# An accumulation of exponentials put behind the background piece of its step

## The chip, the cores and the metric

The kernel runs on one core of one Trainium2 chip. The metric is the device time of one execution in microseconds; less is better. The kernel before took 2945.7 us (median of three runs, 2944.8 to 2946.02).

## The reference, cut to what matters

Four layers of attention over images of 64 x 64 positions with 64 channels, four images, all in fp32. Layer 0 normalises over the keys and sums over the queries, layer 1 has 8 channels for keys and queries and pools its keys, and layers 2 and 3 are the ones that the change touches. Both begin with a group norm, have 4096 queries and 4096 keys per image, and end with a projection and a residual:

```python
# layer 2
q = linear_last(xn, Wq, bq); k = linear_last(xn, Wk, bk); v = linear_last(xn, Wv, bv)
w = jnp.einsum('bchw,bcHW->bhwHW', q, k) * scale
w = jax.nn.softmax(w.reshape(B, H, W, H * W), axis=-1).reshape(B, H, W, H, W)
out = linear_last(jnp.einsum('bhwHW,bcHW->bchw', w, v), Wp, bp) + residual
# layer 3
attn = jnp.einsum('bhwc,bHWc->bhwHW', q, k) * scale
attn = jax.nn.softmax(attn.reshape(B, H, W, H * W), axis=-1).reshape(B, H, W, H, W)
out = h + (jnp.einsum('bhwHW,bHWc->bhwc', attn, v) @ wp + bp)
```

The softmax needs the sum of the exponentials over the keys for each query. That sum, before it is folded over partitions, is what the line of the change computes.

## The kernel before, in words

**Units and steps.** `attention` (L1271) does layers 2 and 3 of one image. It has NC = 4 chunks c of queries times NB = 32 blocks j of keys, 128 units u. `first(u)` (L1282) lets TensorE compute the scores of a unit into an `s` buffer of 128 x 1024 in PSUM (L1287), ScalarE take the exponential into a buffer `p` in SBUF (L1292), and VectorE add `p` to the running sum `zacc` of the chunk (L1298); for j = 0 there is nothing to add. `then(u)` (L1314), two steps later or more, multiplies `p` with the values into two accumulators in PSUM (L1322). At the end of a chunk ScalarE copies one accumulator (L1331) and VectorE adds the other (L1332). There are two `s` buffers, four accumulators, and 14 `p` buffers, used in rotation.

**Order by hand.** The schedule is manual: each engine's instructions stand in the order in which Python issues them. A step (L810) does two units: it calls `first(2t)` and `first(2t+1)`, then the first `then` that is due, then `advance(MID)` (L819), then the second `then`, in the midst of which it may call `advance(LATE)`; then it issues what was put into the list `later`, and last `advance(END)`. `first` issues the add of the odd unit into `later`, and that of the even unit at once. So the order on VectorE within a step is: the even unit's add, the MID piece, the sum of accumulators if there is one, and out of `later` the odd unit's add and, at the end of a chunk, the transpose of `zacc` (L1306) and its reduction (L1310).

**Background pieces.** While the attention of one image runs, the preparation of another runs behind it, cut into pieces by generators that yield the place at which the next piece may go: MID, ALONE, LATE or END. `background` (L779) starts such a generator with a tempo, which is added to a credit in each step; a piece costs one credit (`ready`, L794, and `advance`, L800). The preparation of layer 0 is `before0`, of layer 2 `before2` (its normalising pieces and L1418, L1438 with their evacuations L1423 and L1443), of layer 3 `before3` (means and variances by `summed`, L1353 and L1354, the square L1498 that ScalarE takes of what VectorE wrote in L1496, the projection and the values L906 and L910). Layer 1 as a whole (`layer1`, L1060) is such a background: its score units go to LATE (L1118, L1124) with their own accumulation on VectorE (L1133), its beginning and end to MID and ALONE. A piece that uses TensorE takes one of the two `s` buffers, so that the scores of a later unit wait until the piece's result has been read out of it.

**Urgent pieces.** The end of each chunk puts two entries into `urgent`: `turn` (sums over partitions by L1241, L1246 and L1249, transpose and division L1261 with L1254 or L1268), two steps later, and `last` (layer 2: projection L1466 and residual L1472; layer 3: L1531, L1542 and the stores), two or four steps after it. `advance(MID)` takes an urgent entry that is due ahead of any other piece, and then no LATE piece goes into that step.

**Stages.** After a first stage the order is: layer 0 of image 1 with layers 1 and 2's preparation of image 0; layer 2 of image 0 with layer 1 of image 1; and so on. In the profile the eight stages of layers 2 and 3 begin at 531.7, 1030.9 and 1530.4 us (layer 2, with layer 1 of the next image behind them), 1803.8 and 2028.6 (layer 3), 2255.9 (layer 2), 2481.6 and 2708.4 (layer 3, the last without background).

Of the kernel before, what the change touches and what calls it, by code (L numbers as in the profile page):

```python
# [597 lines left out]
def fast_path(tc: tile.TileContext, a: dict, out: bass.AP, bad, read_flag):  # L598
# [21 lines left out]
    MID, ALONE, LATE, END = range(4)  # L620
# [152 lines left out]
    now = [0]  # L773
    due, before, urgent = {}, {}, []
    later = []
# [18 lines left out]
    def ready(place):  # L794
        at = back["at"]
        if place == LATE and back["alone"] == now[0]:
            return False
        return back["credit"] >= 1.0 and (at == place or place == MID and at == ALONE)

    def advance(place):  # L800
        if place == MID and urgent and urgent[0][0] <= now[0]:
            back["alone"] = now[0]
            urgent.pop(0)[1]()
        elif ready(place):
            if back["at"] == ALONE:
                back["alone"] = now[0]
            back["credit"] -= 1.0
            back["at"] = next(back["gen"], None)

    def step(first=None):  # L810
        back["credit"] = min(back["credit"] + back["tempo"], 3.0)
        for f in before.pop(now[0], ()):
            f()
        if first is not None:
            first()
        work = due.pop(now[0], [])
        for n, f in enumerate(work[:2]):
            if n == 1:
                advance(MID)  # L819
            split = n == 1 and ready(LATE)  # L820
            f(lambda: advance(LATE)) if split else f()
        for f in work[2:]:
            f()
        if len(work) < 2:
            advance(MID)
            advance(LATE)
        passes = list(later)
        later.clear()
        for f in passes:
            f()  # L830
        advance(END)
        now[0] += 1
# [7 lines left out]
    def parts(within, whole):  # L840

        if within is None or whole:
            yield slice(0, 512)
            if within is not None:
                within()
        else:
            yield slice(0, 256)
            within()
            yield slice(256, 512)
# [406 lines left out]
    def turn(o, zsums, spread):  # L1256


        t = o_tile("turned") if spread is None else p_tile()[:, 0:512]
        r = sums(zsums)[1]  # L1260
        nc.vector.transpose(t, o)  # L1261
        if spread is None:
            divide(blocked(t), t, r)
            return t
        u = o_tile("turned")
        split = lambda t: t.rearrange("p (j n f) -> p j n f", n=2, f=32)
        r = r.rearrange("p (j n) -> p j n", n=2).unsqueeze(3).to_broadcast([P, 8, 2, 32])
        nc.vector.tensor_tensor(u.rearrange("p (n j f) -> p j n f", n=2, f=32), split(t), r, ALU.mult)  # L1268
        return spread(u)

    def attention(st, last, not_before, name, final=None, spread=None):  # L1271

        q, k, v = st.pop("q"), st.pop("k"), st.pop("v")
        ps, accs, zaccs, zsums, os = {}, {}, {}, {}, {}
        pairs = NC * NB // 2  # L1280

        def first(u):  # L1282
            c, j = divmod(u, NB)
            s = s_tile()
            for i in range(2):
                for e in range(2):
                    nc.tensor.matmul(  # L1287
                        s[half(e), chunk(i)], k[(j + i) % 2][half(i), ds(j // 2 * P + e * C, C)], q[half(i), chunk(c)],
                        start=True, stop=True,
                    )  # L1290
            p = ps[u] = p_tile()
            nc.scalar.activation(p, s, AF.Exp)  # L1292
            if j == 1:
                zaccs[c] = z_p.tile([P, 1024], FP, tag="zacc", name="zacc")
            if j >= 1:

                p0 = ps[u - 1] if j == 1 else zaccs[c]
                add = lambda: nc.vector.tensor_tensor(zaccs[c], p0, p, ALU.add)  # L1298
                later.append(add) if j % 2 else add()
            if j == NB - 1:  # L1300
                later.append(lambda: turn_blocks(c))

        def turn_blocks(c):

            t = p_tile()
            nc.vector.transpose(t, zaccs.pop(c))  # L1306

            def sum_blocks():
                zsums[c] = small.tile([P, 32], FP, tag="zsums", name="zsums")
                nc.vector.tensor_reduce(zsums[c], t.rearrange("p (n k) -> p n k", k=32), AX.X, ALU.add)  # L1310

            later.append(sum_blocks)

        def then(u, within=None):  # L1314
            c, j = divmod(u, NB)
            if j == 0:
                accs[c] = [acc_tile() for _ in range(2)]
            p = ps.pop(u)
            for cols in parts(within, j in (0, NB - 1)):
                for e in range(2):  # L1320
                    for i in range(2):
                        nc.tensor.matmul(  # L1322
                            accs[c][e][half(i), cols], v[half(e), j, :], p[half(e), chunk(i)][:, cols],
                            start=(j == 0), stop=(j == NB - 1),
                        )
            if c == NC - 1 and j == NB - 1 and final is not None:
                final(accs.pop(c), zsums.pop(c))
            elif j == NB - 1:
                o = os[c] = o_tile("o")
                acc = accs.pop(c)  # L1330
                nc.scalar.copy(o, acc[0])  # L1331
                nc.vector.tensor_tensor(o, o, acc[1], ALU.add)  # L1332
                urgent.append((now[0] + 2, lambda: os.update({c: turn(os[c], zsums.pop(c), spread)})))
                end = now[0] + (4 if spread is None else 6)
                urgent.append((end, lambda: last(c, os.pop(c))))
                if c == NC - 1:
                    urgent.append((end, lambda: st.update({name: True})))

        start = now[0]
        for t in range(pairs):  # L1340
            g = max(start + t + 2, not_before + t // 2)
            due.setdefault(g, []).extend([lambda *within, u=u: then(u, *within) for u in (2 * t, 2 * t + 1)])
        for t in range(pairs):
            step(lambda: (first(2 * t), first(2 * t + 1)))
        return 0
# [493 lines left out]
def conv_seq_kernel(tc: tile.TileContext, a: dict, out: bass.AP):  # L1839

    nc = tc.nc
    with tc.tile_pool(name="flag", bufs=1) as flag:
        bad = flag.tile([1, 1], I32, name="bad")
        n_bad = fast_path(tc, a, out, bad, lambda: nc.values_load(
            bad[0:1, 0:1], min_val=0, max_val=128, skip_runtime_bounds_check_because="it is a count of 128 partitions"
        ))
        with tc.If(n_bad > 0):
            general_path(tc, a, out)
# [37 lines left out]
```

## Time and profile before

| | |
|---|---|
| median of three runs | 2945.7 us |
| the profiled execution | 2945.29 us |
| its span, first to last instruction | 2943.1 us |
| mean granted clock of TensorE | 0.999 |
| TensorE busy | 2910.0 us, 99% |
| VectorE busy | 1843.0 us, 63% |
| ScalarE busy | 1925.2 us, 65% |
| GpSimd busy | 33.6 us, 1% |
| DMA | 30.12 MB, mean 10 GB/s |
| stages of layer 2 with layer 1 behind | 273.4 to 273.8 us each |
| other stages of layers 2 and 3 | 224.8 to 227.3 us, the last 234.6 with the end |

PE stands for TensorE's matmuls, PEld for its weight loads, DVE for VectorE, ACT for ScalarE, SP for SyncE. L1298 is line 1298 of the kernel. A group is given as line, engine, operation, result and inputs; its columns are busy time, mean duration in ns, and the idle time of the engine before it with what ended most of that. The table of waits gives, for an engine and line, what it waited for, and then microseconds in total, times, and the longest. A timeline line is start, duration, engine, line, operation; a bracket at its end is the idle time before it. The ends of matmuls are modelled[...], so that short gaps of TensorE are better seen from the starts.

### The profile page before, as it was taken

To read this page: it belongs to the slowest core of one execution; us is meant where nothing else is said; L and a number is where in the kernel's file an instruction comes from. 1 tells how busy PE (TensorE), PEld (TensorE's weight loads), DVE (VectorE), ACT (ScalarE), POOL (GpSimd) and SP (SyncE) were. 2 spreads that over 40 slices of the span, in tenths; PEclk is the share of its full clock that TensorE was granted. 3 is DMA by queue.
4 is the path that set the end of the run, shared out by engine and by line. 5 is a ranking of instruction groups with operands and counts; after the bars stand their busy time and mean duration, and the time that the engine had idled before them with its cause. 6 is when DMAs were issued, how large, how long until landed. Compare 5 with 4: busy or idle time off the path is not lost.

```text
span 2943.1 us, 66611 instructions
## 1 busy us (share of the span) xinstructions
PE 2910.0 (99%) x29349; PEld 1147.8 (39%) x29349; DVE 1843.0 (63%) x2112; ACT 1925.2 (65%) x2769; POOL 33.6 (1%) x32
## 2 busy tenths in 40 slices
PE   9999999999999999999999999999999999999998
PEld 3333235333544433444443334333344344333333
DVE  1211742588731078872017888888988878878877
ACT  6877777665588866567886665555555555555554
POOL 0000000000000000000000000000000000000000
PEclk9999999999999999999999999999999999999999
DMA  2010000000001000000000000000000100000000
GB/s 38 1 30 5 1 2 13 8 5 17 8 5 30 1 5 5 20 7 17 1 1 5 5 22 6 19 5 9 5 19 6 22 5 8 6 19 5 9 5 10
DMA packets 76779, 30.12 MB, mean 10 GB/s; under 512 B 70465, under 2 KB 74561, under 8 KB 75073
## 3 DMA queue, kind: packets, MB, share of 16 engines
q1 hardware_dynamic: 74224, 25.37, 4.6%
q8 instruction: 232, 3.80, 0.5%
q10 hardware_dynamic: 2256, 0.41, 0.1%
q14 instruction: 67, 0.54, 0.1%
HBM read 4.79 MB, written 4.19 MB: 3 GB/s over the span
## 4 chain that ended last, share of the span: by engine, by line
PE 96%; DVE 2%; ACT 1%; issue 0%; DMA 0%; ACTq 0%; DVEq 0%
PE acc L1322 29%; PE s L1287 29%; PE s L994 15%; PE acc L1025 15%; PE s L1118 2%; PE acc L1144 2%; DVE zacc L1298 1%; ACT p L1124 1%; PE s L1144 1%; PE s L906 1%; PE s L1418 0%; PE s L885 0%; PE s L1179 0%; PE s L1090 0%; PE s L1438 0%
## 5 line engine op out<-in xcount | busy, mean ns | idle before, releaser
L1292 ACT ACTIVATE p<-s 128x1024 f32<-128x1024 f32 x1024 | 994.9, 1022 | 684.3 <-PE s L1287 655.6
L1298 DVE TENSOR_TENSOR zacc<-zacc,p 128x1024 f32<-128x1024 f32 x960 | 1173.6, 1222 | 288.1 <-ACT p L1292 240.5
L1322 PE MATMUL acc<-p,v 64*64 64x512 f32 (+1 forms) x8576 | 1017.8, 572 | 0.0
L1322 PEld LDWEIGHTS acc<-p,v 64*64 64x64 f32 x8576 | 347.7, 133 | 541.7 <-issue 541.7
L1025 PE MATMUL acc<-p,vs 64*64 64x512 f32 (+1 forms) x4224 | 513.3, 578 | 0.5 <-ACT vs L1014 0.5
L1004 ACT ACTIVATE p<-s 128x1024 f32<-128x1024 f32 x480 | 487.3, 1016 | 35.0 <-PE s L994 16.2
L1287 PE MATMUL s<-q,k 64*64 64x512 f32 x2048 | 499.4, 590 | 1.7 <-ACT p L1124 1.7
L994 PE MATMUL s<-xT,q 64*64 64x512 f32 x2048 | 488.5, 591 | 3.0 <-DVE v L910 0.9
L994 PE MATMUL s<-xT,q_swapped 64*64 64x512 f32 x2048 | 489.1, 591 | 0.7 <-DVE o L1153 0.7
L1287 PE MATMUL s<-q,xT 64*64 64x512 f32 x2048 | 488.8, 590 | 0.0
L1287 PE MATMUL s<-q,h_swapped 64*64 64x512 f32 x2048 | 480.2, 589 | 1.8 <-DVE mean L1354 0.5
L1287 PE MATMUL s<-q,k_swapped 64*64 64x512 f32 x2048 | 477.7, 590 | 0.1
L1006 DVE TENSOR_REDUCE all_z<-z 128x1 f32<-128x4 f32 x128 | 20.1, 157 | 624.3 <-ACT p L1004 624.0
L1025 PEld LDWEIGHTS acc<-p,vs 64*64 64x64 f32 x4224 | 186.6, 133 | 262.0 <-issue 198.6
L1014 ACT ACTIVATE vs<-v,all_r 64x64 f32<-64x64 f32 x512 | 176.8, 345 | 138.8 <-PE acc L1025 70.4
L994 PEld LDWEIGHTS s<-xT,q_swapped 64*64 64x64 f32 x2048 | 149.8, 133 | 143.7 <-issue 109.5
L1287 PEld LDWEIGHTS s<-q,k_swapped 64*64 64x64 f32 x2048 | 149.1, 133 | 135.1 <-issue 89.0
L1287 PEld LDWEIGHTS s<-q,h_swapped 64*64 64x64 f32 x2048 | 145.2, 133 | 142.4 <-issue 128.5
L1287 PEld LDWEIGHTS s<-q,xT 64*64 64x64 f32 x2048 | 145.3, 133 | 138.0 <-issue 130.2
L994 PEld LDWEIGHTS s<-xT,q 64*64 64x64 f32 x2048 | 149.1, 133 | 126.9 <-issue 95.6
L1287 PEld LDWEIGHTS s<-q,k 64*64 64x64 f32 x2048 | 150.0, 133 | 113.3 <-issue 92.0
L1124 ACT ACTIVATE p<-s 128x1024 f32<-128x1024 f32 x128 | 124.2, 1022 | 80.8 <-PE s L1118 80.8
(218 smaller groups left out, 1315.1 us busy)
## 6 DMA issues: line engine op xcount, KB each, us to landing
k_swapped<-k SPq DMA_DIRECT2D x8, 512.0 KB, 5.4
residual<-turned SPq DMA_DIRECT2D x128, 32.0 KB, 1.8
h_swapped<-xT SPq DMA_DIRECT2D x8, 512.0 KB, 5.8
out_dram<-turned SPq DMA_DIRECT2D x60, 64.0 KB, 2.0
xin<-in_x_dram SPq DMA_DIRECT2D x12, 256.0 KB, 6.6
q_swapped<-q SPq DMA_DIRECT2D x6, 512.0 KB, 5.9
pg<-pg SPq DMA_DIRECT2D x8, 128.0 KB, 2.3
xin<-in_x_dram SPq DMA_DIRECT2D x12, 64.0 KB, 2.3
```

The source lines that it names most:

```text
L906: nc.tensor.matmul(s[half(e), ds(i * 512 + k * C, C)], rhs[half(i), ds((g * 8 + k) * P + e * C, C)], w[half(i), half(i)], start=True, stop ...
L994: nc.tensor.matmul(s[half(e), chunk(i)], queries(m, i, e), k[half(i), chunk(c)], start=True, stop=True)
L1004: nc.scalar.activation(p, s, AF.Exp, accum_out=z)
L1014: nc.scalar.activation(vs[half(e), :], v[half(e), m, :], AF.Copy, scale=rz[half(e), m : m + 1])
L1025: nc.tensor.matmul(acc[c][half(i), cols], vs[half(e), :], ps[2 * t + n][half(e), chunk(i)][:, cols], start=(m == 0 and e == 0), stop=(m == ...
L1118: nc.tensor.matmul(ss[e][half(m), chunk(i)], pgs[0 if e == d else 1][r, ds(n * P + m * C, C)], th[r, chunk(i ^ j)], start=True, stop=True,)
L1124: nc.scalar.activation(pk[e], ss[e], AF.Exp)
L1144: nc.tensor.matmul(acc[quarter(q), :], g[:, k, :], ps[j, k][q // 2][:, chunk(q % 2)], start=(k == 0 or not bank), stop=(k == NK - 1 or not ...
L1287: nc.tensor.matmul(s[half(e), chunk(i)], k[(j + i) % 2][half(i), ds(j // 2 * P + e * C, C)], q[half(i), chunk(c)], start=True, stop=True,)
L1292: nc.scalar.activation(p, s, AF.Exp)
L1298: add = lambda: nc.vector.tensor_tensor(zaccs[c], p0, p, ALU.add)
L1322: nc.tensor.matmul(accs[c][e][half(i), cols], v[half(e), j, :], p[half(e), chunk(i)][:, cols], start=(j == 0), stop=(j == NB - 1),)
```

## The change

The condition that an urgent piece is due gets a name, `urgent_now`. In `first`, the add of an even unit goes into `later` as well if the step's MID place will be taken: by an urgent piece that is due, or by a background piece at MID or ALONE for which there is credit. It then stands behind that piece on VectorE, directly ahead of the odd unit's add. In steps without such a piece the order is as it was. Layers 0 and 1 have their own code for sums and keep it.

```diff
+    def urgent_now():
+        return urgent and urgent[0][0] <= now[0]
+
     def advance(place):
-        if place == MID and urgent and urgent[0][0] <= now[0]:
+        if place == MID and urgent_now():
             back["alone"] = now[0]
             urgent.pop(0)[1]()
         elif ready(place):
...
                 p0 = ps[u - 1] if j == 1 else zaccs[c]
                 add = lambda: nc.vector.tensor_tensor(zaccs[c], p0, p, ALU.add)
-                later.append(add) if j % 2 else add()
+                later.append(add) if j % 2 or urgent_now() or ready(MID) else add()
```

## The prediction

> **What bounds the kernel now.** I read the page first: the busy times, the chain that ended last, and the two groups that the change concerns.
>
> ```profile
> PE 2910.0 (99%) x29349; PEld 1147.8 (39%) x29349; DVE 1843.0 (63%) x2112; ACT 1925.2 (65%) x2769; POOL 33.6 (1%) x32
> ...
> PE 96%; DVE 2%; ACT 1%; issue 0%; DMA 0%; ACTq 0%; DVEq 0%
> ...
> L1292 ACT ACTIVATE p<-s 128x1024 f32<-128x1024 f32 x1024 | 994.9, 1022 | 684.3 <-PE s L1287 655.6
> L1298 DVE TENSOR_TENSOR zacc<-zacc,p 128x1024 f32<-128x1024 f32 x960 | 1173.6, 1222 | 288.1 <-ACT p L1292 240.5
> ```
>
> TensorE is 99% busy and is 96% of the chain. VectorE is 2% of it, and it can only be worth removing where TensorE waits for VectorE. Second, the table of stages, of which I show a layer 2 stage that has layer 1 behind it and a layer 3 stage (columns: length, then busy time of PE, PEld, DVE, ACT, POOL, clock, DMA).
>
> ```profile
> 1530.40:1803.80 273.40, 272.83 (x2888) 100.68 (x2884) 221.90 (x218) 168.47 (x187) 1.46 (x1) 1.00 0.04 9
> 2481.60:2708.40 226.80, 225.37 (x2264) 85.98 (x2260) 184.94 (x182) 131.35 (x138) 1.46 (x1) 1.00 0.05 11
> ```
>
> VectorE is busy for 81 to 82% of both, TensorE for over 99%. A step of an undisturbed stretch is 3.43 us: four groups (two of scores, two of values) of eight matmuls at 0.86 us. Third, the waits within 2482 to 2709 us, to see what the last 1% is.
>
> ```profile
> PEld s L1241 <- ACT p L1292: 2.4, 4, 1.5
> PEld s L1287 <- DVE v L910: 1.8, 2, 1.3
> ACT sq L1498 <- DVE xT L1496: 1.8, 2, 1.6
> PEld s L1287 <- DVE var L1354: 1.3, 1, 1.3
> ```
>
> The next scores (L1287) wait for VectorE to read a background piece's result out of one of the two `s` buffers: never for an add of L1298 itself. Fourth, the timeline of one such place.
>
> ```profile
> 2055.31 0.27 PE L1353 MATMUL s<-stat,avg 64*64 64x32 f32 x8
> ...
> 2056.28 0.60 PE L1287 MATMUL s<-q,xT 64*64 64x512 f32 x2
> ...
> 2056.39 1.22 DVE L1298 TENSOR_TENSOR zacc<-zacc,p 128x1024 f32<-128x1024 f32 x1 [0.46 <-DVE zacc L1298]
> ...
> 2057.53 0.21 DVE L1354 TENSOR_REDUCE mean<-s 128x32 f32<-128x64 f32 x1
> ...
> 2057.80 0.65 PE L1287 MATMUL s<-q,h_swapped 64*64 64x512 f32 x2 [0.48 <-DVE mean L1354]
> ```
>
> The piece's matmuls ended at 2055.58, but the first unit's add stood ahead of the reduce, which came at 2057.53. The second unit's scores should have begun 0.86 after the first's (2057.14) and began at 2057.80: 0.66 lost. The bracket says 0.48 only, as the ends of matmuls are modelled; I take losses from starts.
>
> [...] the reduce waited 1.95 us with its input ready. [...] Here two adds in a row start 1.32 us apart (2053.38 to 2054.71), an add and an unrelated operation 1.14 (2056.39 to 2057.53).[...]
>
> **The change, part by part.**
>
> *The helper* `urgent_now` only names a test: no instruction. *The condition* adds and removes no instruction either. It moves one add of 1.22 us (even units, j of 2 to 30) behind the MID piece of the same step, where one is due; in other steps nothing moves. ScalarE's and TensorE's orders, the DMAs and the queues of SP and POOL keep theirs; DMAs that follow a VectorE result can only be issued earlier.
>
> *What it takes away.* The losses of the eight stages of layers 2 and 3, each from the distance of the starts of L1287's two groups of eight, less 0.86, and what I expect of each when the piece goes first:
>
> - mean at 2056: 0.66 lost. VectorE without the add is free at about 2056.1, the reduce ends at 2056.3, before 2057.14. All goes: 0.66.
> - v (L910) at 2614.93: 1.43 less 0.86 is 0.57. Its matmuls end at 2614.25; two adds from the turn before hold VectorE to 2614.4; it ends at 2615.6, the buffer is wanted at 2615.8. All goes: 0.57.
> - L1241 at 2551.05 in place of 2550.24: 0.81. Here ScalarE's square (L1498) waited for xT (L1496), which stood behind an add, and the exponentials behind the square. xT moves from 2548.15 to about 2546.9, the square ends by 2548.8, when scores are there. All goes: 0.81.
> - var at 2562.49: 1.48 less 0.86 is 0.62. VectorE is busy without a break from 2551 on (turn 1.8, last 2.1, adds), so that only part of the moved 1.22 arrives, and TensorE comes 0.8 earlier: I count 0.55.
> - v (L1443) at 2169.27: 0.66 lost. Its predecessor (2160.95) waits for its matmuls (2160.8) with or without the add. From there to the next v lie two v (1.2), four adds (5.0) and one last (2.06): 8.2, so it starts at 2169.1 and not 2169.37: 0.27.
> - 14 of the 16 `last` of layer 2 (L1466, two reads of 0.70): second scores late by 0.24 (718.03), 0.23 (1217.24), 0.20 (1716.75), 0.30 (1277) and 0.05 to 0.16 in ten others, 1.9 in all. Without the add the reads would start 0.07 after the matmuls end, as the v of 1233 does: 0.25 earlier in the first three (1216.63, not 1216.89), 0.07 to 0.10 earlier in the others. In the first three all of the loss goes (0.67), in the ten small ones about two thirds (0.7), at 1277 0.07: 1.4.
> - small ones (a square at 1845, q and k at 2153, v at 2161): 0.2.
>
> Sum: 0.66 + 0.57 + 0.81 + 0.55 + 0.27 + 1.4 + 0.2 = 4.5 us. TensorE is the bound, so that each counts once and whole.
>
> *What it adds: a wait.* A piece whose VectorE operation reads a matmul or a square now waits with the moved add queued behind it. In the step of 1057 us the pooled maximum (L1093) begins at 1059.86, when its matmuls end, while the add before ran from 1058.34 in time that is now idle. So up to 1.2 us of VectorE's time is lost per such step, and 0.18 (1.32 less 1.14) where the two adds now stand in a row. With some 25 to 30 pieces in a stage of 64 steps this is at most 36 us, against 42 us idle in the layer 3 stage (226.8 less 184.9) and 52 in the layer 2 one. Behind the waiting instruction stand only the two adds and, every 16 steps, a transpose and a sum. Who waits for these: the exponential that reuses the p buffer, 14 allocations later (seven steps alone, over three with layer 1's), and the sums of L1241, where zsums ends at 2541.7 and is read at 2551. An add delayed by 1 to 3 us reaches neither. And a piece never comes later than before: what stands ahead of it is the same queue, less one add. I take the cost as 0; the bound above is a p buffer that comes late, priced below; below nothing it cannot be, as nothing is removed.
>
> *What is late next:* the pieces end 0 to 0.2 us before the buffer is wanted, except the v at 2169 (0.4 still late) and the last at 1277 (0.2).
>
> **Result of the sum.** The profiled execution took 2945.29 us, its span 2943.1 and 2.2 around it. Less 4.5 this is 2940.8; the median of the runs is 0.4 above the profiled one, so 2941.2, 0.15% faster. About 0.2% (5.9 us) is what a measurement of this kernel can tell from no change; the forecast is below that.
>
> **Rivals.**
>
> - *The wait only changes its name.* Where VectorE is loaded without a break, as from 2551 to 2566, the piece finds VectorE still at the adds that were put off a step before, as at 2169, where 0.27 of 0.66 was left by my count. If this holds for var, the v of 2614 and the lasts too, 2.0 is left (mean, square and the rest): 2943.7. The same result, nearly, if the test is true in few of the steps where the loss is. For it: the idle VectorE time in those stretches is small. Against: mean and square are clear of it.
> - *All waits go.* The losses listed sum to 0.66+0.57+0.81+0.62+0.66+1.9+0.2 = 5.4; what all runs of sixteen L1287 take over 1.72 in the eight stages is 5.8, and the square 0.8: 6.6 at most. Then 2939.1. Against: the v of 2169.
> - *Slower: the idle time in front of a waiting piece makes adds late for the p buffers.* Place: the layer 2 stages with layer 1, where each step takes four p buffers and VectorE does four adds (4.9 us) in a step of 5.64. It decides from the point at which an add is over three steps late. If in each of the three stages eight exponentials then waited 0.5 us, that is 12 us, less 4.5: 2953.2. Against: ScalarE shows no wait for VectorE in these stages but the squares, and urgent pieces keep layer 1's units out of their step (`alone`), which gives VectorE time to catch up.
>
> **How the numbers follow.** Forecast (3 to 5.9 us gained) 0.57; waits renamed (0 to 3) 0.15; all waits go (over 5.9) 0.21; slower 0.07. So faster 0.21, within 0.2% 0.72, slower 0.07. The range 2938.8 to 2944.6 leaves out the slower case and half of the renamed one, with 0.5 of scatter between runs below.
>
> **What would show it.** Right: in the changed trace the mean near 2056, the var near 2560 and the v near 2614 start as their matmuls end, and L1287's second group follows the first by 0.86; VectorE's busy time is unchanged within 2 us; L1298 waits longer for L1292 or for nothing nameable. Wrong: ScalarE waiting for zacc of L1298 in the layer 2 stages (slower), or the same L1287 waits for the same pieces at the same size (renamed). It would be wrong altogether if the moved adds stood elsewhere than directly behind a piece.

## The result, and the profile after

| | before | changed |
|---|---|---|
| median of 20 runs each | 2946.45 us (2944.8 to 2947.43) | 2941.59 us (2940.43 to 2942.68) |
| ratio, 95% interval | | 0.9984 [0.9978, 0.999] |
| the profiled execution, its span | 2945.29, 2943.1 us | 2942.68, 2940.5 us |
| first scores of layer 2's first stage to the start of the closing matmul of the last stage | 531.7 to 2934.4: 2402.7 us | 533.1 to 2930.8: 2397.6 us |

The change takes 4.86 us off, 0.16%, where 4.5 were forecast: 2941.59 us against 2941.2. The interval lies on the side of a gain, but the gain is under the 0.2% that the prediction set as the least that counts. The two profiled executions differ by 2.6 us only, since they differ at their ends, which the change doesn't touch: the changed one is 1.4 us behind at the first mark of the last row (its first scores of all begin at 13.0 us in place of 9.9), and what follows the second mark takes 9.8 in place of 8.8. Between the marks the difference is 5.0, and all of it lies in the eight stages of layers 2 and 3.

First the page of the changed kernel: busy times, the chain, and the two groups (all lines of the code have moved down by 3, so that L1287 is L1290, L1298 is L1301).

```profile
PE 2910.9 (99%) x29349; PEld 1169.8 (40%) x29349; DVE 1846.6 (63%) x2112; ACT 1923.4 (65%) x2769; POOL 33.6 (1%) x32
...
PE 97%; DVE 1%; ACT 1%; SPq 0%; issue 0%; DMA 0%; ACTq 0%; DVEq 0%
...
L1295 ACT ACTIVATE p<-s 128x1024 f32<-128x1024 f32 x1024 | 993.7, 1022 | 687.7 <-PE s L1290 654.9
L1301 DVE TENSOR_TENSOR zacc<-zacc,p 128x1024 f32<-128x1024 f32 x960 | 1173.2, 1222 | 182.6 <-ACT p L1295 119.3
```

The counts are those of before, as nothing was added. The busy times are close to those of before: VectorE has 3.6 us more, the weight loads 22.0. VectorE's share of the chain falls from 2 to 1%. The idle time in front of the add falls from 288.1 to 182.6 us; that is no gain in itself. The table of what VectorE waits for, over the whole run of the changed kernel, shows where it went.

```profile
DVE zacc L1301 <- ACT p L1295: 127.6, 150, 2.8
...
DVE v L913 <- PE s L909: 27.5, 13, 4.6
DVE pg L1096 <- PE s L1093: 21.0, 7, 5.3
```

An add used to wait 248.8 us for its exponential, and the v and the pooled maximum 13.1 and 5.0 us for their matmuls. Now the pieces wait, with the adds behind them. This is the wait that the prediction said the change would add, and it is off TensorE's path. Next the two stages that were shown of before, in the table of stages (length, then busy PE, PEld, DVE, ACT, POOL, clock, DMA).

```profile
1530.90:1803.90 273.00, 272.44 (x2888) 100.52 (x2884) 222.64 (x218) 168.26 (x187) 1.46 (x1) 1.00 0.04 9
...
2480.20:2704.70 224.50, 224.50 (x2260) 89.99 (x2256) 185.28 (x182) 131.12 (x138) 1.46 (x1) 1.00 0.05 11
```

The layer 3 stage is 2.3 us shorter (226.8 before) and TensorE is busy for all of it; the layer 2 stage is 0.4 shorter. Within 2478 to 2706 us of the changed kernel the waits that answer to those shown of before are these.

```profile
PEld s L1244 <- ACT p L1295: 1.3, 4, 0.4
PEld s L1290 <- DVE v L913: 1.2, 2, 0.7
...
PEld s L1290 <- DVE var L1357: 0.6, 1, 0.6
...
ACT sq L1501 <- DVE xT L1499: 0.4, 2, 0.2
```

The var is down from 1.3 to 0.6, the square from 1.8 to 0.4, and the turn's sums (L1241, now L1244) from 2.4 to 1.3. What is left are waits of weight loads (PEld). The starts of the matmuls behind them show what they cost: the scores at the var and the turn's sums come without loss, the scores at the v 0.03 us late. Last, the place that was shown of before, in the timeline of the changed kernel.

```profile
2055.15 0.30 PE L1356 MATMUL s<-stat,avg 64*64 64x32 f32 x8
...
2056.12 0.62 PE L1290 MATMUL s<-q,xT 64*64 64x512 f32 x2
...
2056.79 0.22 DVE L1357 TENSOR_REDUCE mean<-s 128x32 f32<-128x64 f32 x1
2056.97 2.55 DVE L1301 TENSOR_TENSOR zacc<-zacc,p 128x1024 f32<-128x1024 f32 x2
...
2057.08 0.65 PE L1290 MATMUL s<-q,xT 64*64 64x512 f32 x2
```

The reduce now stands ahead of the adds, and the second group of scores comes 0.96 us after the first, where it came 1.52 after: 0.10 is lost in place of 0.66. But the reduce did not start when its matmuls ended, at about 2055.4, nor some 0.2 before the first scores (2056.1 against 2056.28) as forecast. It started 0.67 after them. The prediction missed why; the experiments below look for it.

### The profile page after: what moved, and what is told of

Same layout as the page of the kernel before. It is cut to its first block, busy times and chain, and to the rows that moved or that the text cites. A ratio compares the mean times of both kernels' runs of the same rounds, so it can differ in the third digit from the quotient of the medians.

```text
span 2940.5 us, 66599 instructions
## 1 busy us (share of the span) xinstructions
PE 2910.9 (99%) x29349; PEld 1169.8 (40%) x29349; DVE 1846.6 (63%) x2112; ACT 1923.4 (65%) x2769; POOL 33.6 (1%) x32
## 3 DMA queue, kind: packets, MB, share of 16 engines
HBM read 4.79 MB, written 4.19 MB: 3 GB/s over the span
## 4 chain that ended last, share of the span: by engine, by line
PE 97%; DVE 1%; ACT 1%; SPq 0%; issue 0%; DMA 0%; ACTq 0%; DVEq 0%
PE acc L1325 30%; PE s L1290 30%; PE acc L1028 15%; PE s L997 15%; PE s L1121 2%; PE acc L1147 2%; ACT p L1127 1%; PE s L1147 1%; DVE zacc L1301 0%; PE s L888 0%; PE s L909 0%; PE s L1421 0%; PE s L1093 0%; PE s L1182 0%; PE s L1469 0%
## 5 line engine op out<-in xcount | busy, mean ns | idle before, releaser
L1295 ACT ACTIVATE p<-s 128x1024 f32<-128x1024 f32 x1024 | 993.7, 1022 | 687.7 <-PE s L1290 654.9
L1301 DVE TENSOR_TENSOR zacc<-zacc,p 128x1024 f32<-128x1024 f32 x960 | 1173.2, 1222 | 182.6 <-ACT p L1295 119.3
L1325 PEld LDWEIGHTS acc<-p,v 64*64 64x64 f32 x8576 | 356.4, 133 | 532.9 <-issue 529.2
L1290 PE MATMUL s<-q,k 64*64 64x512 f32 x2048 | 498.0, 590 | 1.7 <-ACT p L1127 1.7
L1290 PE MATMUL s<-q,xT 64*64 64x512 f32 x2048 | 490.2, 589 | 0.0
L1290 PE MATMUL s<-q,h_swapped 64*64 64x512 f32 x2048 | 479.3, 589 | 0.2 <-DVE v L1446 0.2
L1290 PE MATMUL s<-q,k_swapped 64*64 64x512 f32 x2048 | 476.2, 590 | 0.0
L1290 PEld LDWEIGHTS s<-q,h_swapped 64*64 64x64 f32 x2048 | 150.1, 133 | 135.4 <-issue 127.5
L1290 PEld LDWEIGHTS s<-q,xT 64*64 64x64 f32 x2048 | 150.5, 133 | 133.2 <-issue 127.4
L1290 PEld LDWEIGHTS s<-q,k_swapped 64*64 64x64 f32 x2048 | 149.9, 133 | 132.8 <-issue 88.3
L1290 PEld LDWEIGHTS s<-q,k 64*64 64x64 f32 x2048 | 150.2, 133 | 112.7 <-issue 94.2
```

The costliest lines, as they stand in the source:

```text
L1290: nc.tensor.matmul(s[half(e), chunk(i)], k[(j + i) % 2][half(i), ds(j // 2 * P + e * C, C)], q[half(i), chunk(c)], start=True, stop=True,)
L1325: nc.tensor.matmul(accs[c][e][half(i), cols], v[half(e), j, :], p[half(e), chunk(i)][:, cols], start=(j == 0), stop=(j == NB - 1),)
```

## The experiments

The measure in all of them is the loss of TensorE: what a run of sixteen matmuls of L1290 takes over 1.72 us (two groups of 0.86), counted from the first start to the start of the values behind them, and summed over the eight stages. It is about 5.8 us before and 1.8 after (good to about 0.1, since 1.72 is rounded). With the 0.81 us of the late turn near 2551, which is a loss ahead of such a run, the change gains some 4.0 + 0.8 = 4.8 by this measure; the medians differ by 4.86.

The kernel before was measured again beside the experiments, with medians of 2946.39, 2946.53 and 2946.25 us; the ratios below are to these. The first theory was the prediction's: each piece gains for itself when the add of its step is moved behind it, and nothing else changes. The rivals were that a late add costs something, and that less of VectorE's work, and not the order, is what helps.

**Only in urgent steps, only in other steps.** The condition has two parts. Each was tried alone.

```diff
-                later.append(add) if j % 2 or urgent_now() or ready(MID) else add()
+                later.append(add) if j % 2 or urgent_now() else add()
```

> The even add goes behind urgent pieces only (turn, last); behind other MID pieces it stays ahead. Theory (each place where the piece's read of an s buffer comes earlier gains by itself): the losses at the 14 `last` go, about 1.7 us, and the mean, the square, the var and the two v keep most of theirs; about 2944.5 us, ratio 0.9993 to the kernel before, 1290's second groups after L1356 and L909 still 0.4 to 0.7 late. Rival (the parts need each other, VectorE must be relieved in all steps of a loaded stretch): no more than 0.5 us, 2946.

```diff
-                later.append(add) if j % 2 or urgent_now() or ready(MID) else add()
+                later.append(add) if j % 2 or (not urgent_now() and ready(MID)) else add()
```

> The even add goes behind credited MID and ALONE pieces only, not behind urgent ones. Theory: mean 0.6, square 0.8, var about 0.6, v 0.6 and 0.2 are gained, some 2.8 us, the losses at the `last` of layer 2 stay (about 1.9): 2943.5 us, ratio 0.999. Urgent-only and this one add up to the whole change, 4.9 us. Rival (parts need each other): the two together fall short of it by over 1.5 us.

Measured: 2950.46 us for the urgent part alone, 1.0013 [1.0006, 1.002], and 2950.69 for the other part alone, 1.0014 [1.0008, 1.0021]. Both expected gains are losses, of 4.1 and 4.3 us: each half of the change makes the kernel slower, and the two together make it faster. The losses of the runs of sixteen are about 9.3 and 10.9 us. So the parts do not add up, and the theory of separate gains falls. The rival, that the parts need each other, was right, though it too expected no loss. VectorE's timeline with the urgent part alone, at the mean of 2056, shows what happens:

```profile
2052.57 0.69 DVE L1545 TENSOR_TENSOR turned<-turned,residual 128x512 f32<-128x512 f32 x1
2053.18 5.21 DVE L1301 TENSOR_TENSOR zacc<-zacc,p 128x1024 f32<-128x1024 f32 x4
2058.84 1.23 DVE L1301 TENSOR_TENSOR zacc<-zacc,p 128x1024 f32<-128x1024 f32 x1 [0.46 <-DVE zacc L1301]
2059.99 0.22 DVE L1357 TENSOR_REDUCE mean<-s 128x32 f32<-128x64 f32 x1
```

and VectorE's timeline of the changed kernel at the same place:

```profile
2051.06 0.69 DVE L1545 TENSOR_TENSOR turned<-turned,residual 128x512 f32<-128x512 f32 x1
2051.67 5.21 DVE L1301 TENSOR_TENSOR zacc<-zacc,p 128x1024 f32<-128x1024 f32 x4
...
2056.79 0.22 DVE L1357 TENSOR_REDUCE mean<-s 128x32 f32<-128x64 f32 x1
```

The `last` (it ends with L1545) is an urgent piece. Its own add was moved behind it, and so four adds stand between it and the mean, where the kernel before has three and the mean's own as the fourth. With the urgent part alone the mean's own is still in front, as a fifth: the mean starts 2.19 us after the first scores behind its matmuls (2057.80), against 1.25 before, and 1.65 us of TensorE are lost there in place of 0.71. In the changed kernel the fifth is gone, the mean stands behind four, as before, and starts 0.67 after the first scores. That is 0.58 earlier than before, though the queue ahead of it is no shorter: against the scores the row of adds began 0.23 earlier, and from there to the mean it took 5.12 us in place of 5.47, as VectorE does not stand still in it. The moved add is a **debt**: it has left the place ahead of one piece for the place ahead of the next, and is paid only if the next piece also goes ahead of its own add. The second half shows the same from the other side, in VectorE's timeline near the `last` of 1220 us:

```profile
1216.20 1.24 DVE L943 STREAM_TRANSPOSE xT<-xin 128x1024 f32<-128x1024 f32 x1
1217.36 3.84 DVE L1301 TENSOR_TENSOR zacc<-zacc,p 128x1024 f32<-128x1024 f32 x3
1221.12 1.29 DVE L1475 SCALAR_TENSOR_TENSOR xT<-s,bp,xT 128x256 f32<-128x256 f32 x2
```

The transpose of layer 1 (L943) went ahead of its add, and its add, the odd unit's and then that of the `last`'s own step stand in a row in front of the `last`. In the kernel before there were two adds there. TensorE's second scores come 1.25 us late, in place of 0.23. The `last` pieces lose 6.4 us in all, where they lost 2.1 before, and the turns, the other urgent pieces, lose 3.3 us where they lost nothing.

**Two tests of the debt.** In urgent steps the even add is left out and not moved, so that nothing can be owed.

```diff
-                later.append(add) if j % 2 or urgent_now() or ready(MID) else add()
+                if j % 2:
+                    later.append(add)
+                elif not urgent_now():
+                    add()
```

> Urgent-only, but in the steps of urgent pieces the even unit's add is left out altogether in place of being moved (some 60 of 992 adds, the sums of the softmax of layers 2 and 3 lack those keys); credited pieces have the add ahead. Debt theory: with nothing put off, the next pieces are no worse than in the kernel before, and the `last` gain: 2943 to 2944.7 us, 6 us or more under urgent-only, the mean of about 2057 not over 0.7 late. Rival: as urgent-only, about 2950.

Measured: 2942.26 us, 0.9986 [0.9979, 0.9992]: 8.2 us under the urgent part alone, and a little under what was expected. VectorE's timeline of this kernel at the mean:

```profile
2054.58 1.23 DVE L1301 TENSOR_TENSOR zacc<-zacc,p 128x1024 f32<-128x1024 f32 x1 [1.24 <-ACT p L1295]
2055.72 0.22 DVE L1360 TENSOR_REDUCE mean<-s 128x32 f32<-128x64 f32 x1
```

The mean's own add is still in front of it, and nothing is lost, since that add waits for its exponential alone. So at this place an add in front does harm only when the queue behind the earlier piece is already long. But this kernel also takes work away: 63 adds, and 75 us of VectorE's busy time (1771.3 in place of 1846.6). Alone it cannot tell a debt that is not made from a load that is lighter. A second test, which leaves nothing out, moves the add of a non-urgent step only if an add was moved within the two steps before, that is, where a debt is open.

```diff
+    moved = [-9]
...
-                later.append(add) if j % 2 or urgent_now() or ready(MID) else add()
+                behind = j % 2 == 0 and (urgent_now() or ready(MID) and now[0] - moved[0] <= 2)
+                if behind:
+                    moved[0] = now[0]
+                later.append(add) if j % 2 or behind else add()
```

> Urgent-only, and besides that the add goes behind a credited piece if an add was moved at most two steps earlier. New theory (a debt): an add that is moved behind one piece stands in front of the next piece, which is then three adds deep unless its own step's add moves too; urgent-only lost 3.4 us that way. Here each piece soon after a moved add moves its own: the losses of urgent-only at the mean (1.6), the var (1.3) and the v (1.5, 1.2) go, 2942 to 2943.5 us, ratio about 0.9987. Rival (urgent-only was slow for some other cause, as in its start or in the urgent steps themselves): it stays near 2950.

Measured: 2941.91 us, 0.9986 [0.9979, 0.9992], as the theory of the debt expected. The same 992 adds are done as in the urgent part alone, and its loss of 4.1 us has become a gain of 4.3. By the order of VectorE's instructions in the traces the change places 181 adds elsewhere than before, 58 in urgent steps and 123 in others; this kernel places 159. So it is not far from the whole change, and shows that the other 22 moves are not needed.

**Order or load.** The even adds are left out altogether (the sums then lack those keys).

```diff
-                later.append(add) if j % 2 or urgent_now() or ready(MID) else add()
+                later.append(add) if j % 2 else None
```

> Leaves out the adds of the even units altogether (480 of 992, the sums of the softmax of layers 2 and 3 lack those keys); the odd adds stay behind the piece. VectorE has some 590 us less to do. Theory: only the order bound the kernel, not what VectorE can carry; what the change left of losses behind VectorE (0.46 at the v of 2168, 0.3 at the last of 1277, 0.1 twice) goes too, about 0.9 us: 2940.7, ratio 0.998. Rival (VectorE's load bounds the loaded stretches): 5 us or more under the changed kernel.

Measured: 2941.18 us, 0.9981 [0.9973, 0.9989]. VectorE does 577 us less (1270.0 in place of 1846.6), and the kernel is 0.4 us under the changed one, no difference that these runs can tell. So once the order is right, taking half of the adds away brings no more that these runs can tell. In its trace the 0.46 us at the v of 2168 are gone, but the 0.30 at the `last` of 1278 stays, which had been expected to go. And the order alone decides much: with all 992 adds in five different orders the medians are 2941.6 (changed), 2946.4 (before), 2950.5, 2950.7 and, below, 3011.3 us.

**The other extreme.** Both units' adds are issued ahead of the piece.

```diff
-                later.append(add) if j % 2 or urgent_now() or ready(MID) else add()
+                add()
```

> Both adds of a step go ahead of the piece: the suspected cost doubled. Theory: a piece then cannot be read before the odd unit's exponential and its add are done, about 4.4 us after the step begins; against when the buffer is wanted this is late by 1.0 at each of 16 `last` of layer 2, by 0.2 at 29 turns, by 0.5 at some 40 pieces with matmuls: 30 to 40 us slower than the kernel before, 2981, ratio 1.011 to 1.014, all of it in waits of the scores for VectorE. Rival (the place of the adds on VectorE matters little, the gain has another source): within 2 us of the kernel before.

Measured: 3011.25 us, 1.022 [1.0206, 1.0234]: 64.9 us slower. The direction was right, the size was not: 30 to 40 had been expected. TensorE's scores now wait for many pieces, with far larger times; these are lines of its table of waits.

```profile
PE s L1290 <- DVE xT L1475: 16.0, 14, 1.5
PE s L1290 <- DVE all_z L1249: 9.3, 28, 1.0
...
PE s L1290 <- DVE v L913: 3.9, 7, 0.8
```

The turns' sums (L1249) had no place in this table for the kernel before, where only weight loads waited for them, 7 times and 1.9 us in all; with a second add ahead of them the scores wait 28 times. The losses of the runs of sixteen sum to about 62 us, 56 more than before: most of the 64.9. The expectation had counted too little: its own terms, 16 for the `last`, 29 times 0.2 for the turns and 40 times 0.5, sum to 42, and the turns alone lose 15.8, over 0.5 each.

**Late in every step.** The even add always goes behind, with a piece or without.

```diff
-                later.append(add) if j % 2 or urgent_now() or ready(MID) else add()
+                later.append(add)
```

> The even add always goes into the late list, with or without a piece in the step. In steps without a piece nothing of VectorE stands between the two places but the sum of two accumulators at the end of a chunk. Theory: the same as the changed kernel within 0.5 us, 2941.6, ratio 0.9984, and the same losses left (about 1.7 us over all runs of sixteen scores). Rival (a late add hurts, and the test keeps that small): slower than the changed kernel by more than 1 us.

Measured: 2943.95 us, 0.9991 [0.9982, 0.9999], 2.4 us slower than the changed kernel. Here the rival was right: a late add can cost. Three places carry 1.6 of it, the `last` pieces of 652, 1151 and 1651 us with 0.52 to 0.53 each; the other 0.8 has no place in the trace. The source is 30 us earlier, at the end of a chunk; VectorE's timeline of the always-late kernel:

```profile
623.28 0.69 DVE L1335 TENSOR_TENSOR o<-o,acc 128x512 f32<-128x512 f32 x1 [6.29 <-ACT o L1334]
623.89 5.13 DVE L1301 TENSOR_TENSOR zacc<-zacc,p 128x1024 f32<-128x1024 f32 x4
...
631.21 0.18 DVE L1249 TENSOR_REDUCE all_z<-s 128x16 f32<-128x32 f32 x1
...
651.99 1.26 DVE L1475 SCALAR_TENSOR_TENSOR xT<-s,bp,xT 128x256 f32<-128x256 f32 x2
```

and the same in the changed kernel:

```profile
618.25 1.22 DVE L1301 TENSOR_TENSOR zacc<-zacc,p 128x1024 f32<-128x1024 f32 x1
624.45 0.69 DVE L1335 TENSOR_TENSOR o<-o,acc 128x512 f32<-128x512 f32 x1 [4.98 <-ACT o L1334]
625.06 3.88 DVE L1301 TENSOR_TENSOR zacc<-zacc,p 128x1024 f32<-128x1024 f32 x3
...
631.72 0.19 DVE L1249 TENSOR_REDUCE all_z<-s 128x16 f32<-128x32 f32 x1 [0.52 <-PE s L1244]
...
652.59 1.27 DVE L1475 SCALAR_TENSOR_TENSOR xT<-s,bp,xT 128x256 f32<-128x256 f32 x2
```

The sum of accumulators waits for ScalarE's copy at the head of the queue. In the changed kernel one add goes ahead of it, in time that would be idle; always late, it stands behind, and VectorE loses 1.31 us more there. The lateness can be followed to the `last`. The always-late kernel reaches this place 1.17 us earlier than the changed one, by its sum of accumulators as by its later matmuls; with that taken off, VectorE is 1.26 us late behind the four adds. The 0.52 us for which it waits ahead of the turn (L1249) in the changed kernel are used up, so that it is 0.66 late there. From there to the `last` (L1475) VectorE has no break in either kernel, and starts the `last` 0.57 late, of which 0.53 reaches TensorE. The trace has the same course at 1123 to 1152.

**Moving this wait, and moving the adds further.** In the changed kernel the sum of accumulators itself was put behind the piece:

```diff
-                nc.vector.tensor_tensor(o, o, acc[1], ALU.add)
+                later.append(lambda: nc.vector.tensor_tensor(o, o, acc[1], ALU.add))
```

> The changed kernel, with the sum of the two accumulators at the end of a chunk put into the late list behind the step's adds, where VectorE stood still for up to 5 us before it. Theory: this idle time decides nothing once the adds that need it are in front (it cost 0.5 us three times only in always-late), so 2941.6 within 0.7 us; at the last of 1277 nothing changes. Rival (the standstill is what leaves VectorE short in the layer 2 stages): 1 us or more under the changed kernel. A loss would mean that an accumulator came free too late.

Measured: 2941.43 us, 0.9983 [0.9977, 0.999], the same as the changed kernel: where one add goes ahead of the sum, its wait costs nothing that these runs can tell. And all adds, even and odd, were held back until the next step's MID place had been passed:

```diff
+    held = []
+    def flush():
+        passes = list(held)
+        held.clear()
+        for f in passes:
+            f()
...
             if n == 1:
                 advance(MID)
+                flush()
...
-        passes = list(later)
+        held.extend(later)
         later.clear()
-        for f in passes:
-            f()
+        if back["at"] is None:
+            flush()
...
-                later.append(add) if j % 2 or urgent_now() or ready(MID) else add()
+                later.append(add)
```

> All adds wait for a whole step more: they are issued behind the MID place of the step after, while there is a background. Theory: nobody waits for an add but the p buffer seven steps (three with layer 1) on and the sums two steps on, so 2941.6 within 1 us, ratio 0.9984; the v of 2168 keeps its 0.4, since the work of VectorE between two such pieces is the same. Rival (late adds hold up p buffers or the sums): slower than the changed kernel by 3 us or more, in exponentials that wait for zacc.

Measured: 2941.25 us, 0.9982 [0.9974, 0.999], no different from the changed kernel. The v of 2169, which the changed kernel left late, keeps its 0.46 here too. VectorE stands for 6.29 us ahead of the sum of accumulators near 624 us in this kernel as well, and the `last` of 652 loses nothing: only two adds follow, and then 4.19 us are idle ahead of the turn. So it is not the wait at the sum by itself that costs, but what is put behind it with no idle time left before the next piece.

**Fewer `p` buffers.** The prediction's slower rival was an add that holds a `p` buffer too long. Both kernels ran with 11 of them in place of 14.

```diff
-    x_p, p_p, z_p, o_p = pool("x", 13), pool("p", 14), pool("z", 2), pool("o", 2)
+    x_p, p_p, z_p, o_p = pool("x", 13), pool("p", 11), pool("z", 2), pool("o", 2)
```

> The changed kernel with 11 buffers p in place of 14. Theory: the moved add is 1 to 3 us later, a rotation of 11 is 2.7 steps with layer 1 and 5.5 without, so that what 11 buffers cost is the same with and without the change: this and the next differ by 4 to 5.5 us in favour of the change. The cost of 11 buffers itself is not known, 0 to 20 us. Rival (late adds): the difference shrinks below 2 us or turns round.

> The kernel before with 11 buffers p in place of 14, the counterpart of the run before. Theory: 4 to 5.5 us slower than that; rival: less than 2 us slower, or faster.

Measured: 2999.05 us with the change, 1.0177 [1.0163, 1.0191], and 3002.68 us without it, 1.0188 [1.0174, 1.0202]. The kernels with 11 buffers lose some 56 us, all of it ahead of layer 2's first stage, in layers 0 and 1. The mean granted clock over the whole run is lower too, 0.990 with the change and without where it is 0.999 with 14; how much of the 56 us that makes was not worked out. With 11 buffers the change is still worth 3.6 us, a little less than expected. An add that comes later within its step, with three buffers fewer, shows no cost here: in the table of waits, read down to 13.6 us in all, no exponential of L1295 waits for it. How few it takes was not tried.

## Why the prediction was right, and where it was wrong

**The bound** was read rightly: TensorE, and of VectorE's work only what stands ahead of a piece that holds an `s` buffer: 577 us of adds less brought 0.4 us, which these runs can't tell from nothing. All sizes below are losses of runs of sixteen, before and after, except that of the turn.

| step | forecast gain | loss before, after | gain |
|---|---|---|---|
| mean, 2056 | 0.66 | 0.71, 0.13 | 0.58 |
| v (L910), 2615 | 0.57 | 0.62, 0 | 0.62 |
| turn and square, 2551 | 0.81 | gone: L1244 starts 0.86 after its predecessor | 0.81 |
| var, 2562 | 0.55 | 0.68, 0 | 0.68 |
| v (L1443), 2169 | 0.27 | 0.69, 0.46 | 0.23 |
| `last` of layer 2 | 1.4 | 2.17, 0.51 | 1.66 |
| small ones | 0.2 | | 0.25 |
| sum | 4.5 | | 4.83 |

These losses, too, are good to some 0.05 us each. Every term came within 0.3 us, the v of 2169 among them, whose queue had been counted through. The prediction put its start at 2169.1. The changed kernel reaches this place 0.86 us earlier (first scores at 2168.41 in place of 2169.27), which makes it 2168.24; VectorE's timeline of the changed kernel has it behind the two adds of the step before:

```profile
2165.81 2.55 DVE L1301 TENSOR_TENSOR zacc<-zacc,p 128x1024 f32<-128x1024 f32 x2
2168.27 1.28 DVE L1446 TENSOR_TENSOR v<-s,bv 128x512 f32<-128x512 f32 x2
```

It starts at 2168.27. Its matmuls begin at 2166.69 and the next on TensorE at 2167.55: the v is 0.7 late, and 0.46 of that reaches TensorE. This is the one place where the rival of renamed waits was right. For var and the rest it was wrong: var lost nothing more, so the 0.07 kept back for it was too cautious.

**The step that failed** is the sentence that a piece never comes later than before, since what stands ahead of it is the same queue less one add. It is the same queue less one add, plus the adds moved out from ahead of earlier pieces. The mean shows it: I had VectorE free at 2056.1 and it was free at 2056.79, with the `last`'s moved add in front. "Each counts once and whole" failed with it, as the two half changes show, which are slower by 4.1 and 4.3 us where that sum gives gains. The total still came out because all pieces move their adds: what a piece gets from its predecessor and what it passes on nearly cancel. At the mean the agreement of 0.66 and 0.58 is luck: its queue is as long as before, and it gained by a standstill of VectorE that was gone (0.35) and a row of adds that began 0.23 earlier. The prediction had the debt at hand. It counted the put-off adds for the two v and named them in its rival of renamed waits, but not for the mean, and not as a rule. The expectations for the halves were worked out the same way and had the wrong sign.

**The cost of the added wait**, taken as 0, held: no exponential's wait for an add cost TensorE anything, and with 11 buffers none was seen. The table of waits of the changed kernel puts seven waits of exponentials down to an add, 10.2 us in all (3 and 3.6 before). They are in stages without layer 1, none is longer than the 1.5 us for which ScalarE waits there for its scores anyway, and no scores are late there. Here too the reason given was too wide. That the bound was idle time of VectorE does not make all of it free: always late, 1.31 us of VectorE's time at the end of a chunk became some 0.53 us of TensorE's, three times.

**The rivals.** "All waits go" (2939.1) fell short by the v of 2169 (0.46), the `last` pieces of 779 and 1278 (0.07 and 0.30), and by losses that the change doesn't touch (0.31 in all behind the scores of layer 1, L1118, 0.14 behind L1160, 0.12 in runs followed by L1025; lines of the kernel before). "Slower" was not seen in the change, but its kind exists, as the always-late kernel shows, by another mechanism than the buffers: the queue behind a wait. What was to be followed through is that the reduce, with its input ready, did not pass the add issued ahead of it. The trace of the changed kernel has the same for a piece behind an earlier one: the mean's matmuls had ended at 2055.45 by their modelled ends, and VectorE came to it at 2056.79, 1.34 us later, behind four adds.

**Signs asked for.** The mean, the var and the v of 2615 were to start as their matmuls end. None did: they started 1.34, 1.26 and 0.21 us after the modelled ends, each directly behind moved adds, and yet (nearly) in time. This sign would have told of the debt at once. VectorE's busy time was to stay within 2 us: it rose by 3.6 (1843.0 to 1846.6), of which the stage of 1531 has 0.7; the groups of L1301 are the same (1173.6 and 1173.2), and the rest was not followed. The add (L1301) was to wait longer for its exponential: it waits 127.6 us in place of 248.8, since the pieces now wait ahead of it. The sign of a slower kernel, exponentials that wait for the add in the stages with layer 1, did not appear.

## What to carry to other kernels

To move an instruction behind a critical one does not remove it: it then stands ahead of the next critical one, as here the four adds ahead of the mean, which VectorE came to 1.34 us after its matmuls. Count the queue from one critical instruction to the next, with the debts of all earlier moves in it. Where a moved instruction would stand ahead of the next critical one, move that one's own as well, or move neither; half the rule cost here nearly what the whole rule gained (4.1 and 4.3 us against 4.9). And put the moved work where its engine would wait anyway, not where no idle time is left before the next critical instruction (always late, 0.53 us of TensorE's time lost at each of three places).

## What the runs showed of the hardware

- VectorE stood still for 0.46 us ahead of an add whose inputs had been written: at 2056.39 in the kernel before, where ScalarE's last exponentials had ended at 2055.78, and at 2058.84 in the urgent half, where they, a pair, had run from 2055.36 to 2057.30. The profile names the add before, which had ended. Of the 0.58 us that the mean gained, this standstill is the larger part (0.35, as even without it two adds in a row are 1.33 apart), as it is absent from the changed kernel at this place. What causes it was not found.
- Two profiled executions began differently: the first scores started at 9.9 and 13.0 us, and 1.4 us of this was left at layer 2's first stage. The change is worth 4.9 us, so that stage lengths and medians say more than the spans of two single executions.
